# Keys and values of a head pair as seven block products in a gated cross-attention kernel, with the projections placed by due dates

## The chip, the cores and the metric

The kernel runs on one core of a Trainium2 chip. The time is the device time of one execution in microseconds. A run of several executions gives a median. One further execution was taken with the hardware profiler: the page and the trace are of that execution. TensorE does the matmuls, VectorE and ScalarE the elementwise work, POOL is GpSimd, and SP issues most of the DMAs.

## The reference, cut to what matters

```python
# x (4, 256, 512), ctx (4, 1601, 512); 32 query heads, 8 key/value heads, head size 128; all fp32
xn = layernorm(x)
q = (xn @ Wq + bq)                        # 4 query heads to one key/value head
k, v = split(ctx @ Wkv + bkv)             # 8 heads of 128 each
attn = softmax(q k^T / sqrt(128))
x = x + tanh(g_xattn) * (attn v @ Wo + bo)
x = x + tanh(g_ffn) * ffn(layernorm(x))   # base product, router over 8 experts, two rank-16 experts a token
```

## The kernel before

The work is a list of 4 x 8 key/value heads, `heads`. A head has two *groups*, `(b, h, l)`: group l holds 128 of the 256 tokens for the head's four query heads, 512 columns in all. The 1601 context tokens are 13 row tiles: twelve of 128 and one of 65. They are handled as seven "pairs", the short tile first.

**A group.** `run_group(cur, prev)` scores the current group and weights the values of the previous one, in turn. `score_unit` (L442) multiplies `kT` with `qT` into a score bank `sc`, and ScalarE copies it to a tile `p` (L449); `fold` keeps a running maximum on VectorE (L389 to L394). `av_unit` (L492) multiplies the exponentials of the previous group with `v` into the one bank `av`; at its end VectorE and ScalarE write `oT` (L502, L503). `AHEAD` says how many units the scores lead the values. After the group `softmax` spreads the maximum over the partitions (`spread`, L396 to L415), subtracts it on VectorE in seven instructions (L464) and takes the exponential on ScalarE (L465). The sums of the exponentials (`sum_unit`, again `fold` and `spread`) belong to the next call of `run_group`.

**Between two groups** comes what this document calls a *window*: the work that is not attention proper. Keys of a head come in four chunks of 400 or 401 tokens, four contraction blocks of 128 each (`pk`, L311), evacuated by ScalarE with the bias (L318). Queries come in four items (`pq`, L330, L337). Values of a head pair are made tile by tile, 256 columns for the two heads (`pv`, L363, L370). The output projection `po` (L515) follows its group and is added to `xa` by VectorE (L522). At the change of a batch the context is loaded and transposed into `ctxT` (L145, L146), and the feed-forward steps run.

**The order.** TensorE's order is the program's order (`manual_schedule`); other engines are ordered by a scheduler that looks at which instruction is ready and, among those, at which comes first in the program. A small planner writes TensorE's order. Work is cut into steps with a cost in ns and a lag before they may run (`LAG_O`, 6 us, between a group and its `po`). A `Task` is a list of such steps. `run_group` slips in steps of at most 432 ns (transposes) between units; `fill(share)` runs steps in list order until a share of all open cost is used up, 1/2 after the first group of a head and all after the second; `flush` then finishes what the next head needs.

**Memory.** PSUM has three score banks (`ps_sc`), one for `av` and four for all else (`ps`, `bank()`). `p` has `NPAIR + AHEAD + 1` = 10 buffers. `wk` is loaded twice ahead, `wv`, `wq` and `wo` once; loads wait on the SP queue for their buffer.

Of the kernel before, what the change touches and what calls it, by code (L numbers as in the profile page):

```python
# [27 lines left out]
def flamingo_kernel(  # L28
# [35 lines left out]


    nc = tc.nc
    B, L, D = x.shape
# [15 lines left out]
    NPAIR = len(pairs)  # L83
    AHEAD = 2
    n_chunks = -(-LK // 512)
    base, extra = divmod(LK, n_chunks)
    chunks, s = [], 0
    for i in range(n_chunks):
# [6 lines left out]
    small = ctx.enter_context(tc.tile_pool(name="small", bufs=4))  # L95
    ps_sc = ctx.enter_context(tc.tile_pool(name="ps_sc", bufs=3, space=bass.MemoryType.PSUM))
    ps_av = ctx.enter_context(tc.tile_pool(name="ps_av", bufs=1, space=bass.MemoryType.PSUM))
    ps = ctx.enter_context(tc.tile_pool(name="ps", bufs=4, space=bass.MemoryType.PSUM))

# [70 lines left out]

    def load_wk(b, h, eng=nc.sync):
        k = pool.tile([P, NC, HDIM], F32, tag="wk", name=f"wk_{b}_{h}")
        eng.dma_start(
            k, wkv[:, h * HDIM : (h + 1) * HDIM].rearrange("(c p) f -> p c f", p=P)
        )
        w_t["k", b, h] = k

    def load_wv(b, hp, eng=nc.sync):
        v = pool.tile([P, NC, 2 * HDIM], F32, tag="wv", name=f"wv_{b}_{hp}", bufs=1)
        lo = KVD + hp * 2 * HDIM  # L180
        eng.dma_start(v, wkv[:, lo : lo + 2 * HDIM].rearrange("(c p) f -> p c f", p=P))
        w_t["v", b, hp] = v

# [48 lines left out]

    xa_t, xnT_t, ctxT_t = {}, {}, {}
    STAGE = 3

# [31 lines left out]
    def ctx_steps(b):  # L267

        staged = {}

        def load(i):
            s = pool.tile([P, D], F32, tag="stage", name=f"ctx_{b}_{i}", bufs=STAGE)
            nc.sync.dma_start(s[: rows[i]], ctx_kv[b, i * P : i * P + rows[i], :])
            staged[i] = s

        def begin():
            ctxT_t[b] = pool.tile([P, NC, LK], F32, tag="ctxT", name=f"ctxT_{b}", bufs=1)
            for i in range(STAGE - 1):
                load(i)

        def step(i):
            def run():
                if i + STAGE - 1 < KT:
                    load(i + STAGE - 1)
                turn_ctx(b, i, staged.pop(i))
            return NC * TR_COST, LAG_CTX, run

        return [(0, 0, begin)] + [step(i) for i in range(KT)]

# [11 lines left out]

    def qk_steps(b, h):
        def begin():
            qT_t[b, h] = pool.tile([P, G, L], F32, tag="qT", name=f"qT_{b}_{h}")
            kT_t[b, h] = pool.tile([P, LK], F32, tag="kT", name=f"kT_{b}_{h}")

        def k_item(s, n):
            def run():
                pk = bank(f"pk_{b}_{h}_{s}")
                for c in range(NC):  # L310
                    nc.tensor.matmul(  # L311
                        pk[:, :n],
                        w_t["k", b, h][:, c, :],
                        ctxT_t[b][:, c, s : s + n],
                        start=(c == 0),
                        stop=(c == NC - 1),
                    )
                nc.scalar.activation(  # L318
                    kT_t[b, h][:, s : s + n],
                    pk[:, :n],  # L320
                    AF.Identity,
                    bias=bias_of("k", h),
                )
            return NC * mm_cost(n), 0, run

        def q_item(g):
            def run():
                pq = bank(f"pq_{b}_{h}_{g}")
                for c in range(NC):
# [7 lines left out]
                nc.scalar.activation(  # L337
                    qT_t[b, h][:, g, :],
                    pq[:, :L],
                    AF.Identity,  # L340
                    bias=bias_of("q", h * G + g),
                )
            return NC * mm_cost(L), 0, run

        return [(0, 0, begin)] + [k_item(s, n) for s, n in chunks], [q_item(g) for g in range(G)]

    def v_steps(b, hp):

        WV = 2 * HDIM

        def v_begin():
            v_t[b, hp] = pool.tile([P, KT, 2, HDIM], F32, tag="v", name=f"v_{b}_{hp}")

        def v_item(i):
            n = 2 if i + 1 < KT and rows[i + 1] == P else 1
            r = rows[i]

            def run():
                pv = bank(f"pv_{b}_{hp}_{i}")
                for j in range(n):  # L360
                    s = (i + j) * P
                    for c in range(NC):
                        nc.tensor.matmul(  # L363
                            pv[:r, j * WV : (j + 1) * WV],
                            ctxT_t[b][:, c, s : s + r],
                            w_t["v", b, hp][:, c, :],
                            start=(c == 0),
                            stop=(c == NC - 1),
                        )
                nc.scalar.copy(  # L370
                    v_t[b, hp][:r, i : i + n].rearrange("p j t f -> p (j t f)"), pv[:r, : n * WV]
                )
            return n * NC * mm_cost(WV), 0, run

        starts, i = [], 0
        while i < KT:
            starts.append(i)
            i += 2 if i + 1 < KT and rows[i + 1] == P else 1
        return [(0, 0, v_begin)] + [v_item(i) for i in starts]


# [150 lines left out]
    def ffn_steps(b, l):  # L532
# [17 lines left out]
        def pick(p, tag):  # L550
# [6 lines left out]
            return v, oh  # L557

        def route_item():
            pm = bank(f"pm_{nm}")  # L560
            WR = E * R + E
            for c in range(NC):
                nc.tensor.matmul(
                    pm[:, :WR], box["xT"][:, c, :], ra[:, c, :], start=(c == 0), stop=(c == NC - 1)
                )
            py = bank(f"py_{nm}")
            for c in range(NC):
                nc.tensor.matmul(py, box["xT"][:, c, :], base_t[:, c, :], start=(c == 0), stop=False)  # L568
            box["py"] = py
            lm = pool.tile([P, WR], F32, tag="lm", name=f"lm_{nm}")  # L570
# [34 lines left out]

        def final_item():
            py = box["py"]
            nc.tensor.matmul(py, box["midT"], lb, start=False, stop=True)
# [6 lines left out]
            (NC * TR_COST, LAG_NORM, turn_item),  # L615
            (NC * (mm_cost(E * R + E) + mm_cost(D)), LAG_COPY, route_item),
            (TR_COST, LAG_ROUTE, mid_item),
            (mm_cost(D), LAG_COPY, final_item),
        ]

# [6 lines left out]
    class Task:  # L627


        def __init__(self, steps, head=None):  # L630
            self.steps = deque(steps)
            self.head = head
            self.ready = clock["now"] + self.steps[0][1]
# [49 lines left out]

    def fill(share):

        credit = share * sum(t.cost() for t in tasks)
        while tasks and credit > 0:
# [7 lines left out]
            else:  # L695
                break

    ctx.enter_context(tc.manual_schedule(engines={mybir.EngineType.PE}))
# [11 lines left out]
    load_first(0)  # L710
    load_wk(*heads[0], nc.scalar)
    load_first(1)
    load_small()
    load_first(2)
    load_first(3)
    load_wv(0, 0)
    xs = x_steps(0, 0)
# [4 lines left out]
    ctxT_t[0] = pool.tile([P, NC, LK], F32, tag="ctxT", name="ctxT_0", bufs=1)  # L722
    ks, qs = qk_steps(*heads[0])
    ks.pop(0)[2]()
    vs = v_steps(0, 0)
    vs.pop(0)[2]()
    ends = [s + n for s, n in chunks]
# [15 lines left out]
    for f in xs + vs + qs:  # L743
        f[2]()
    load_wk(*heads[1])
    load_wq(*heads[1])
    load_wo(*heads[0])
    tasks.append(Task(ffn_weight_steps()))

    prev = None  # L750
    for hi, (b, h) in enumerate(heads):
        if hi + 2 < len(heads):
            load_wk(*heads[hi + 2])
        nxt = heads[hi + 1] if hi + 1 < len(heads) else None
        if h % 2 == 0:
            if h + 2 < NKV:
                load_wv(b, h // 2 + 1)
            elif b + 1 < B:
                load_wv(b + 1, 0)
            halves = v_steps(b, h // 2 + 1) if h + 2 < NKV else []  # L760
        if nxt is not None:
            ks, qs = qk_steps(*nxt)
            if nxt[1] == 0:
                tasks.append(Task(x_steps(nxt[0], LAG_NORM), nxt))
                tasks.append(Task(ctx_steps(nxt[0]) + ks + qs + v_steps(nxt[0], 0), nxt))
            else:
                tasks.append(Task(ks + qs, nxt))
        if halves:
            n = len(halves) // 2 if h % 2 == 0 else len(halves)
            tasks.append(Task(halves[:n], nxt))  # L770
            halves = halves[n:]
        for l in range(NL):
            cur = (b, h, l)
            if cur == last:
                break
            fill(0)
            run_group(cur, prev)
            if prev is not None:
                tasks.insert(0, Task(out_steps(prev)))
            prev = cur  # L780
            if nxt is not None:
                fill(1.0 / (NL - l))
        flush(lambda t: t.head == nxt and nxt is not None)
        if hi + 2 < len(heads):
            load_wq(*heads[hi + 2])

# [56 lines left out]
```

## Time and profile before

| | |
|---|---|
| median of 3 runs | 2713.86 us (2712.91 to 2722.68) |
| the profiled execution | 2717.0 us, span 2715.2 us |
| clock granted to TensorE | 0.994 |
| scores L442, values' weighting L492 | 1664 passes each, mean 594 and 592 ns |
| keys L311, values L363, queries L330 | 1024, 1664 and 1024 passes |
| HBM | 104.52 MB moved, 38 GB/s |

A group's line in the profile gives line, engine, operation, output and inputs with shapes, count, then busy time and mean duration, then the engine's idle time just before these instructions and what ended it. A matmul's duration holds a drain that overlaps the next matmul, so durations of TensorE don't add up; starts do. Each fp32 matmul of the code appears as two passes in the trace, each with a weight load (PEld).

### The profile page before, as it was taken

The numbers are of one execution on the slowest core, as the hardware profiler recorded it, in microseconds if no ns is written. First come the engines' busy times: TensorE is split into PE (matmuls) and PEld (weight loads), VectorE is DVE, ScalarE is ACT, GpSimd is POOL, SyncE is SP. The second block draws the span as 40 slices with busy tenths as digits, with TensorE's granted clock in tenths as the row PEclk, the third lists the DMA queues.
The fourth block names the chain that finished last, engine by engine and source line by source line (L and its number), as shares of the span: only waits on it lengthen the run. The fifth ranks groups of instructions, "written<-read, shape, count | busy, mean of one in ns | idle before, by whom it ended". The sixth has DMA issues, their size and how long they took to land.

```text
span 2715.2 us, 22496 instructions
## 1 busy us (share of the span) xinstructions
PE 2672.2 (98%) x7997; PEld 1478.2 (54%) x7997; DVE 2006.6 (74%) x3093; ACT 1178.8 (43%) x1821; POOL 6.2 (0%) x21
## 2 busy tenths in 40 slices
PE   8999999999999999999999999999999999999998
PEld 6555555555655555555555555555555555555543
DVE  1977777786768777778676787787866768777787
ACT  2543443454444434435443444444544444434442
POOL 0000000000000000000000000000000000000000
PEclk9999999999999999999999999999999999999999
DMA  4110110112001101011200110110210011100000
GB/s 156 41 35 28 35 31 28 43 43 76 25 23 54 35 20 43 16 43 58 61 28 20 55 35 22 40 35 24 72 35 28 20 47 35 35 27 32 19 13 24
DMA packets 69800, 104.52 MB, mean 38 GB/s; under 512 B 3068, under 2 KB 27692, under 8 KB 69688
## 3 DMA queue, kind: packets, MB, share of 16 engines
q1 hardware_dynamic: 68808, 102.27, 11.7%
q8 instruction: 63, 1.03, 0.2%
q0 software_dynamic: 272, 0.53, 0.1%
q14 instruction: 49, 0.40, 0.1%
q10 hardware_dynamic: 608, 0.29, 0.0%
HBM read 100.98 MB, written 2.10 MB: 38 GB/s over the span
## 4 chain that ended last, share of the span: by engine, by line
PE 94%; DVE 4%; ACT 1%; DMA 1%; issue 0%; SPq 0%; DVEq 0%; ACTq 0%
PE sc L442 26%; PE av L492 24%; PE pv L363 13%; PE pk L311 12%; PE po L515 8%; PE pq L330 8%; DVE p L464 1%; ACT p L465 1%; PE py L568 1%; PE pt_ctx L145 0%; DVE mx L394 0%; DMA ctx<-in_ctx_dram 0%; DVE p_last L464 0%; DVE mx L399 0%; DVE res_mx L413 0%
## 5 line engine op out<-in xcount | busy, mean ns | idle before, releaser
L442 PE MATMUL sc<-qT,kT 128*128 128x512 f32 (+1 forms) x1664 | 769.9, 594 | 6.2 <-ACT p_last L449 3.4
L492 PE MATMUL av<-p,v 65*128 65x512 f32 x1640 | 755.7, 592 | 0.0
L449 ACT COPY p<-sc 65x512 f32<-65x512 f32 x820 | 478.9, 585 | 598.5 <-PE sc L442 598.1
L394 DVE TENSOR_TENSOR mx<-mx,p 128x1024 f32<-128x1024 f32 x252 | 308.3, 1223 | 406.3 <-ACT p L449 405.8
L492 PEld LDWEIGHTS av<-p,v 65*128 65x128 f32 x1640 | 310.0, 190 | 382.3 <-issue 377.5
L442 PEld LDWEIGHTS sc<-qT,kT 128*128 128x128 f32 (+1 forms) x1664 | 307.4, 186 | 381.8 <-issue 359.3
L464 DVE TENSOR_TENSOR p<-p,res_mx 65x512 f32<-65x512 f32 x442 | 472.2, 1135 | 0.1
L465 ACT ACTIVATE p<-p 65x512 f32<-65x512 f32 x442 | 420.0, 989 | 34.0 <-DVE p L464 28.5
L311 PE MATMUL pk<-ctxT,wk 128*128 128x400 f32 (+1 forms) x1024 | 361.8, 506 | 8.5 <-ACT ctxT L146 7.1
L363 PE MATMUL pv<-wv,ctxT 128*128 128x256 f32 (+1 forms) x1664 | 369.1, 379 | 0.0
L363 PEld LDWEIGHTS pv<-wv,ctxT 128*128 128x128 f32 (+1 forms) x1664 | 308.9, 186 | 60.0 <-issue 13.1
L394 DVE TENSOR_TENSOR sm<-sm,p 128x1024 f32<-128x1024 f32 x252 | 307.9, 1222 | 17.0
L311 PEld LDWEIGHTS pk<-ctxT,wk 128*128 128x128 f32 x1024 | 195.5, 192 | 171.1 <-issue 28.6
L515 PE MATMUL po<-wo,oT 128*128 128x512 f32 x512 | 238.3, 609 | 15.2 <-ACT p L465 7.2
L330 PE MATMUL pq<-xnT,wq 128*128 128x256 f32 x1024 | 231.3, 379 | 0.0
L330 PEld LDWEIGHTS pq<-xnT,wq 128*128 128x128 f32 x1024 | 194.6, 190 | 47.8 <-issue 15.4
L503 ACT ACTIVATE oT<-oT,biasT 128x512 f32<-128x512 f32 x64 | 46.2, 722 | 363.8 <-DVE oT L502 363.8
L389 DVE TENSOR_TENSOR mx<-p,p 128x1024 f32<-128x1024 f32 x63 | 76.1, 1208 | 157.0 <-ACT p L449 157.0
L370 ACT COPY v<-pv 128x512 f32<-128x512 f32 (+1 forms) x112 | 61.6, 550 | 253.1 <-PE pv L363 253.1
L515 PEld LDWEIGHTS po<-wo,oT 128*128 128x128 f32 x512 | 99.2, 195 | 125.8 <-issue 96.5
L318 ACT ACTIVATE kT<-pk,biasT 128x400 f32<-128x400 f32 (+1 forms) x128 | 75.2, 587 | 133.2 <-PE pk L311 133.2
L337 ACT ACTIVATE qT<-pq,biasT 128x256 f32<-128x256 f32 x128 | 59.2, 463 | 73.9 <-PE pq L330 73.9
(108 smaller groups left out, 1145.2 us busy)
## 6 DMA issues: line engine op xcount, KB each, us to landing
wq<-in_L_xattn_Wq_dram SPq DMA_DIRECT2D x32, 1024.0 KB, 5.2
wo<-in_L_xattn_Wo_dram SPq DMA_DIRECT2D x32, 1024.0 KB, 5.1
ctx<-in_ctx_dram SPq DMA_DIRECT2D x48, 256.0 KB, 2.7
wv<-in_L_xattn_Wkv_dram SPq DMA_DIRECT2D x16, 512.0 KB, 3.3
wk<-in_L_xattn_Wkv_dram SPq DMA_DIRECT2D x31, 256.0 KB, 3.1
xa<-in_x_dram SPq DMA_DIRECT2D x4, 512.0 KB, 4.1
out_dram<-y SPq DMA_DIRECT2D x8, 256.0 KB, 2.0
base<-in_L_ffn_base_W_dram SPq DMA_DIRECT2D x4, 256.0 KB, 8.3
```

The lines of the kernel that those rows point to most:

```text
L311: nc.tensor.matmul(pk[:, :n], w_t["k", b, h][:, c, :], ctxT_t[b][:, c, s : s + n], start=(c == 0), stop=(c == NC - 1),)
L318: nc.scalar.activation(kT_t[b, h][:, s : s + n], pk[:, :n], AF.Identity, bias=bias_of("k", h),)
L330: nc.tensor.matmul(pq[:, :L], w_t["q", b, h][:, c, g * HDIM : (g + 1) * HDIM], xnT_t[b][:, c, :], start=(c == 0), stop=(c == NC - 1),)
L363: nc.tensor.matmul(pv[:r, j * WV : (j + 1) * WV], ctxT_t[b][:, c, s : s + r], w_t["v", b, hp][:, c, :], start=(c == 0), stop=(c == NC - 1),)
L389: nc.vector.tensor_tensor(acc, p[first], p[first + 1], op)
L394: nc.vector.tensor_tensor(acc, acc, p[j], op)
L442: nc.tensor.matmul(sc[:r, :], kT_t[b, h][:, i * P : i * P + r], qT_t[b, h][:, :, l * P : (l + 1) * P], start=True, stop=True,)
L449: nc.scalar.copy(p[:r, k, :], sc[:r, :])
L464: nc.vector.tensor_tensor(p, p, mb[:r].unsqueeze(1).to_broadcast([r, n, W]), ALU.subtract)
L465: nc.scalar.activation(p, p, AF.Exp, scale=scale)
L492: nc.tensor.matmul(av, v_t[b, h // 2][:r, i, h % 2, :], p_t[key][j][:r, k, :], start=(j == 0 and k == 0), stop=(j == NPAIR - 1 and k == le ...
L515: nc.tensor.matmul(po, oT_t[key][:, g, :], w_t["o", b, h][:, g, :], start=(g == 0), stop=(g == G - 1),)
```

## The change

For the pairs of heads of keys and of values, the two contraction halves (256 of 512), two heads and two halves of the first 1536 tokens (768 each) form a 2 x 2 block product. It is computed in Winograd's form of Strassen's algorithm with seven block products. The sums of weight blocks are made on GpSimd (`weight_sums`), the sums of context blocks on VectorE once a batch (`ctx_sums`, partly in place in `ctxT`). Each product runs on two pieces of 384 tokens, 28 matmuls of 384 columns for keys, 84 matmuls of 128 columns for values. A piece has three PSUM banks: x collects products 1, 6, 5, 3 one after the other and is copied out by ScalarE after each; z holds product 2, y products 7 and 4, and VectorE adds them to what was copied. The last 65 tokens are done plainly in `tail`. Head 0, head 1 and the first pair of values keep the plain form.

The planner's tasks get a due group in place of a head: values of a pair in the window after its own first group, queries mostly in the last window before their head, keys of the next pair spread over three windows (two where a batch begins). `window(now)` gives each task its cost divided by the windows left. Weights of a pair share one buffer `wkv`, loaded by four DMAs. `AHEAD` goes from 2 to 1, the score banks from 3 to 2, `ps` from 4 banks to 5, the staging buffers from 3 to 2. The base product of the feed-forward moves from `route_item` to `final_item` except in the last batch.

```diff
-    AHEAD = 2
+    AHEAD = 1
+    HK = FULL // 2 * P
+    NSUB = -(-HK // 512)
+    SUB = HK // NSUB
+    TAIL = 2 * HK
...
-    ps_sc = ctx.enter_context(tc.tile_pool(name="ps_sc", bufs=3, space=bass.MemoryType.PSUM))
+    ps_sc = ctx.enter_context(tc.tile_pool(name="ps_sc", bufs=2, space=bass.MemoryType.PSUM))
...
-    ps = ctx.enter_context(tc.tile_pool(name="ps", bufs=4, space=bass.MemoryType.PSUM))
+    ps = ctx.enter_context(tc.tile_pool(name="ps", bufs=5, space=bass.MemoryType.PSUM))
...
+    def load_pair(kind, b, hp, tile_=None, eng=nc.sync):
...
+            w = pool.tile([P, 7, 2, HDIM], F32, tag="wkv", name=f"w{kind}_{b}_{hp}", bufs=1)
+        lo = (KVD if kind == "v" else 0) + hp * 2 * HDIM
+        for slot, half, f in ((A11, 0, 0), (A12, 1, 0), (A21, 0, 1), (A22, 1, 1)):
+            eng.dma_start(
...
+    def weight_sums(kind, b, hp):
+        w = w_t[kind, b, hp]
+        for out_, x_, y_, op in (
+            (S1, A21, A22, ALU.add),
+            (S2, S1, A11, ALU.subtract),
+            (S4, A12, S2, ALU.subtract),
+            (S3, A11, A21, ALU.subtract),
+        ):
+            nc.gpsimd.tensor_tensor(w[:, out_], w[:, x_], w[:, y_], op)
...
-    STAGE = 3
+    STAGE = 2
...
+    def ctx_sums(b):
...
+        for s0 in range(0, HK, SUB):
...
+            nc.vector.tensor_tensor(t1, b12, b11, ALU.subtract)
+            nc.vector.tensor_tensor(t2, b22, t1, ALU.subtract)
+            nc.vector.tensor_tensor(t4, b21, t2, ALU.subtract)
+            nc.vector.tensor_tensor(b12, b22, b12, ALU.subtract)
+        nc.vector.tensor_tensor(tt, ct[:, 2:4, TAIL:], ct[:, 0:2, TAIL:], ALU.subtract)
...
+        kT_t[b, h] = pool.tile([P, LK], F32, tag="kT", name=f"kT_{b}_{h}", bufs=3)
...
+        v_t[b, hp] = pool.tile([P, KT, 2, HDIM], F32, tag="v", name=f"v_{b}_{hp}", bufs=1)
...
+        def product(i, s, bk, first):
+            if is_k:
+                for c in range(2):
+                    nc.tensor.matmul(
+                        bk[:, :SUB],
+                        a(SLOT[i], c),
+                        operand(i, c, s, SUB),
...
+            for t in range(SUB // P):
+                for c in range(2):
+                    nc.tensor.matmul(
+                        bk[:, t * HDIM : (t + 1) * HDIM],
+                        operand(i, c, s + t * P, P),
+                        a(SLOT[i], c),
...
+        def add_to(f, half, s, bk):
+            o = place(f, half, s)
+            nc.vector.tensor_tensor(o, seen(bk), o, ALU.add)
...
+                product(i, s, bk, i in (1, 2, 7))
+                if i == 1:
+                    copy_to(0, 0, s, bk)
+                elif i == 2:
+                    add_to(0, 0, s, bk)
+                elif i == 6:
+                    copy_to(1, 0, s, bk)
+                elif i == 5:
+                    copy_to(1, 1, s, bk)
+                    add_to(1, 1, s, banks["y", s])
+                elif i == 3:
+                    copy_to(0, 1, s, bk)
+                elif i == 4:
+                    add_to(1, 0, s, bk)
...
+        for i in (1, 2, 6, 7, 5):
+            steps += [step(i, s) for s in subs]
+        if n:
+            steps.append((2 * NC * mm_cost(P), 0, tail))
+        for i in (3, 4):
+            steps += [step(i, s) for s in subs]
...
-    def fill(share):
+    def window(now):
...
+        credit = sum(t.cost() / (t.due - now + 1 if t.due is not None else 1) for t in tasks)
...
+        flush(lambda t: t.due is not None and t.due <= now)
...
+            if h == NKV - 2 and l == 1 and b + 1 < B:
+                tasks.append(Task(x_steps(b + 1, LAG_NORM), now + 1))
+                tasks.append(Task(ctx_steps(b + 1), now))
             run_group(cur, prev)
             if prev is not None:
                 tasks.insert(0, Task(out_steps(prev)))
             prev = cur
+            if h % 2 == 0 and l == 0 and hi > 0:
+                tasks.append(Task(pair_steps("v", *pair), now))
+            if nxt is not None and l == (0 if h % 2 == 1 and nxt[1] > 0 else NL - 1):
+                tasks.append(Task(q_steps(*nxt), hi * NL + NL - 1))
+            if coming is not None and h % 2 + l == 1 and (l == 1) == (h < NKV - 2):
+
+                tasks.append(Task(pair_steps("k", *coming), (hi | 1) * NL + NL - 1))
             if nxt is not None:
-                fill(1.0 / (NL - l))
+                window(now)
+            if h % 2 == 0 and l == 0 and coming is not None:
+                load_pair("k", *coming)
+                weight_sums("k", *coming)
+            if h % 2 == 1 and l == NL - 1 and coming is not None:
+                load_pair("v", *coming)
+                weight_sums("v", *coming)
```

## The prediction

> **What bounds the kernel now.** I read the page's busy shares first, then the chain that ended last, then the groups by shape, then one undisturbed stretch of the timeline.
>
> ```profile
> span 2715.2 us, 22496 instructions
> PE 2672.2 (98%) x7997; PEld 1478.2 (54%) x7997; DVE 2006.6 (74%) x3093; ACT 1178.8 (43%) x1821; POOL 6.2 (0%) x21
> PE 94%; DVE 4%; ACT 1%; DMA 1%; issue 0%; SPq 0%; DVEq 0%; ACTq 0%
> ```
>
> TensorE is busy 98% of the span and is 94% of the chain. A gain can come only from fewer TensorE passes; a loss from TensorE being made to wait. Price of a pass: durations of matmuls contain a drain that overlaps the next one, so I take runs of equal instructions from the chain in order of time (start, length, what), and the groups for shapes.
>
> ```profile
> 53.59 6.92 PE pq L330 x32
> 201.13 8.63 PE pv L363 x40
> 232.09 8.07 PE pk L311 x24
> L311 PE MATMUL pk<-ctxT,wk 128*128 128x400 f32 x768 | 268.0, 499 | 1.7 <-DVE ctxT L146 1.4 <-ACT ctxT L146 0.3
> L363 PE MATMUL pv<-wv,ctxT 128*128 128x256 f32 x1536 | 340.8, 379 | 0.0
> L563 PE MATMUL pm<-ra,fT 128*128 128x136 f32 x64 | 8.9, 282 | 1.8 <-DVE fT L146 1.8
> L502 DVE TENSOR_TENSOR oT<-av,res_sm 128x512 f32<-128x512 f32 x64 | 41.9, 654 | 0.0
> ```
>
> A pass of 256 columns takes 8.63/40 = 215.8 ns, one of 400 takes 8.07/24 = 336.2: about 0.834 ns a column and 2.2 ns. Counts show two passes for each fp32 matmul of the code (1024 pk = 32 heads x 4 chunks x 4 blocks x 2).
>
> Next, a stretch between two groups, on TensorE and VectorE:
>
> ```profile
> 1013.59 5.31 PE L492 MATMUL av<-p,v 128*128 128x512 f32 x12
> 1018.74 5.34 PE L330 MATMUL pq<-xnT,wq 128*128 128x256 f32 x24
> ...
> 1027.37 3.60 PE L515 MATMUL po<-wo,oT 128*128 128x512 f32 x8
> ...
> 1020.46 7.48 DVE L464 TENSOR_TENSOR p<-p,res_mx 65x512 f32<-65x512 f32 x7
> 1027.86 1.21 DVE L389 TENSOR_TENSOR sm<-p,p 128x1024 f32<-128x1024 f32 x1
> ...
> 1032.38 0.74 DVE L522 SCALAR_TENSOR_TENSOR xa<-po,gates,xa 128x512 f32<-128x512 f32 x1
> 1039.40:1061.80 22.40, 22.40 (x54) 9.86 (x53) 10.49 (x16) 7.97 (x14) 0.00 (x0) 1.00 0.07 24
> ```
>
> When the last av pass of a group has been issued (1018.7), VectorE is occupied with the softmax until 1027.9, 9.1 us into the window; then come the sums. The xa addition, for a po that ended at 1030.8, is put between two sums: work of the window goes behind the subtractions but ahead of the sums. The last line is the following group (busy PE, PEld, DVE, ACT, POOL): VectorE is idle for 12 of its 22.4 us.
>
> Last, what a window costs when PSUM banks run out:
>
> ```profile
> 776.53 1.89 PE L330 MATMUL pq<-xnT,wq 128*128 128x256 f32 x8
> 780.83 3.67 PE L515 MATMUL po<-wo,oT 128*128 128x512 f32 x8 [2.41 <-ACT p L465]
> 773.04 7.48 DVE L464 TENSOR_TENSOR p<-p,res_mx 65x512 f32<-65x512 f32 x7
> 780.44 0.29 DVE L571 COPY lm<-pm 128x136 f32<-128x136 f32 x1
> ```
>
> pm, py, another py and pq held the four banks; their readers stood behind the seven subtractions and the exponentials, and TensorE stood for 2.41 us.
>
> **Passes saved.** Call the four windows of a head pair A, B (even head, l = 0, 1), C, D (odd head). Fifteen of sixteen pairs change, for keys and for values (head 0, head 1 and the first values stay plain).
>
> Keys, a pair: now 64 x 336.2 ns = 21.52 us. After: 7 products x 2 pieces x 2 blocks x 2 passes = 56 of 384 columns, 322.6 ns each by the line above, 18.07; the tail of 65 tokens is 8 matmuls, 16 passes, each bound by its 128-column weight load, which I put at 109: 1.74. Saved: 1.71.
>
> Values, a pair: now 104 x 215.8 = 22.44. After: 7 x 6 x 2 x 2 = 168 passes of only 128 columns, and 16 in the tail, each with a weight load of its own. By the line a pass is 109 ns: 20.06. Saved: 2.38.
>
> Together 4.09 us a pair, 61 us in 15 pairs.
>
> **A rule against it.** The short pass is the risk, because one weight load of 128 columns must hide behind 128 columns of matmul. The nearest row is pm, 136 columns with a load each: its eight passes begin at 726.44 and the next matmul at 727.36, 115 ns a pass, just what the line gives for 136. [...] At 115 the gain falls by 200 x 6 ns x 15 = 18 us, to 43. Nothing excludes a floor between.
>
> **What is added beside TensorE.** VectorE: six additions from PSUM a pair and kind, 128x384. From oT (654 ns at 512) and the folds (1214 at 1024), 1.09 ns a column: 514 ns each, 6.2 us a pair; ctx_sums 8 x 934 ns, 7.7 us a batch. In all 93 + 31 us: VectorE goes from 74% to about 79%. In the windows they delay the sums, which have the group's 12 idle us to end in. ScalarE: eight evacuations of 384 columns in place of eight of 400 or six of 512, and the tails: +1.5 us a pair at 43% load. POOL: four 128x256 operations a load, 30 loads; no row is near. [...]
>
> **Where stalls come.** The pool `ps` has five banks after the change, but a pair (products in the order 1, 2, 6, 7, 5, tail, 3, 4, each on two pieces) holds two x banks from product 1 to 3, two y banks from 7 to 4, and two z banks (product 2) until VectorE adds them. Times below count from the last av pass of the group before.
> - A, the values: products 1, 1, 2, 2, 6 fill 6.5 us, then comes po (its lag is 6 us), then the second 6; at 11.3 us product 7 wants a bank. The z additions can run from 9.1, the first is done by 9.7. No stall, 1.5 us of margin.
> - B: queries first (6.9), po, then five key steps (credit 6.6 us, 1.29 each). No stall.
> - C: key steps 6, 7, 7, 5, 5 (6.45 us), then po takes the fifth bank until 9.9; the tail wants one at once. VectorE leaves the subtractions at 9.1, adds both y (10.2), then xa (10.95): 1.1 us of stall. In 12 pairs: 13 us (the three keys loaded across a batch start in C instead).
> - D: the rest of the keys, then queries, which now come last before a group: L442 shows 0.56 us for a group that begins right behind qT (five times now). 15 x 0.56, less what is there: 7 us.
> - Batch change, three times: TensorE no longer waits for ctxT (2.05 + 0.28, L311 and L515 at 632 and 637): -7. ctx_sums stand before the sums, so the third score tile of group (7,0) waits for its p buffer (AHEAD 1, one buffer fewer): about 2 each, +6. The routing bank plus x and z banks in window A: 3.2 in place of 2.4, +2. Loads of ctx one ahead: 2.7 us to land against 3.9 between steps, hidden.
> - Score tiles in two banks: copy done 1.64 us after a score began, third one due at 1.72. 64 x 0.05 = 3.
> - Start and end: four issues in place of one on two queues, and p_last behind two banks: +2.
>
> Sum +26 us; 61 - 26 = 35. The profiled execution took 2717.0 us for its span of 2715.2, so it would take 2682. The median of the runs is 2713.86, 3.1 below it: 2679.
>
> **Rivals.**
> 1. All of the gain: the waits in C and D fall in other slots, and nothing new stalls: 61 us, 2653. For: the page shows TensorE without a gap in windows as short as 11.5 us. Against: the 2.41 us line.
> 2. Slower, by held banks. If the additions from PSUM are served behind the sums, not ahead of them, z and y stay held until some 21.5 us into A and C instead of 9.7: product 7 in A would stand 10 us, the tail in C 11. From 4.1 us a pair the gain is gone; with 8 us (served halfway) it is +59, 2773. For: readers stood 8 us behind the subtractions (lm). Against: xa at 1032.38 went ahead of the sums.
> 3. Little left: a pass costs 115 ns (a gain of 43) and the stalls are those above: -17, 2697; with 1 us in each of 60 windows in their place, +17, 2731. For: VectorE works through the whole of a window already (1014.4 to 1040.2), and gets more to do there. Against: the group after it gives it time.
> 4. The change does nothing: excluded, the passes are counted in the code.
>
> **How the numbers follow.** Forecast 0.50 (2664 to 2695), rival 1 0.20, rival 3 0.16 (0.08 of it at its good end, 0.06 within the bound, 0.02 slower), rival 2 0.14, a serial weight load being in it. A measurement of this kernel tells some 0.5%, 13.6 us, from no change. Faster 0.50 + 0.20 + 0.08 = 0.78, same 0.06, slower 0.14 + 0.02 = 0.16. The range runs from rival 1 with 5 us of today's stalls gone too, 2648, past the good end of rival 3 to 2708; rival 2 and the rest of 3, together 0.2, stay outside.
>
> **What would show it.** Right: 840 passes of 384 columns for keys and 2520 of 128 for values, runs of the latter at 109 ns; PE busy down by about 55; VectorE near 79%; idle time before the key tail of about 1 us, released by VectorE, and 0.56 before sc. Wrong: pv runs at 115 or more; idle before products 7 of the values; idle before L442 from ScalarE copies of several us a group.

## The result, and the profile after

The changed kernel takes 2752.86 us (median of 4 runs, 2752.24 to 2755.68). Beside it the kernel before took 2713.39 (2711.16 to 2722.68). The ratio is 1.0141, with an interval of 1.0116 to 1.0165: 1.4% slower, where 1.3% faster was forecast. First the page of the changed kernel: span, busy shares, and the chain that ended last by engine.

```profile
span 2750.8 us, 25888 instructions
...
PE 2653.8 (96%) x9317; PEld 1502.2 (55%) x9317; DVE 2149.1 (78%) x3309; ACT 1201.4 (44%) x1881; POOL 166.4 (6%) x141
...
PE 81%; DVE 15%; ACT 2%; issue 1%; DMA 0%; ACTq 0%; DVEq 0%
```

TensorE's share fell from 98% to 96%, and VectorE's part of the chain went from 4% to 15%. So TensorE now stands, and for VectorE. The waits of TensorE (who waits for whom; us in all, times, longest) say where:

```profile
PE ptk L550 <- DVE xa L721: 32.0, 12, 2.7
PE sc L641 <- ACT qT L361: 19.5, 19, 3.5
PE sc L641 <- ACT p L648: 8.0, 5, 3.3
...
PE ptk L550 <- ACT kT L552: 6.1, 15, 0.4
```

The first line, and 15 of the 19 waits of the second, are those that the prediction placed in windows C and D. The timeline of one window C, first TensorE, then VectorE (start, length, what, count, idle time before and who ended it):

```profile
481.57 3.60 PE L691 MATMUL av<-p,v 128*128 128x512 f32 x8
485.01 1.45 PE L455 MATMUL pxk<-T,wk 128*128 128x384 f32 x4
...
491.46 3.60 PE L714 MATMUL po<-wo,oT 128*128 128x512 f32 x8
497.73 1.10 PE L550 MATMUL ptk<-ctxT,wk 128*128 128x65 f32 x8 [2.67 <-DVE xa L721]
499.24 0.66 PE L550 MATMUL ptk<-ctxT,wk 128*128 128x65 f32 x4 [0.41 <-ACT kT L552]
499.73 0.71 PE L550 MATMUL ptk<-T,wk 128*128 128x65 f32 x4
500.24 2.87 PE L455 MATMUL pxk<-ctxT,wk 128*128 128x384 f32 x4
...
488.58 7.50 DVE L663 TENSOR_TENSOR p<-p,res_mx 65x512 f32<-65x512 f32 x7
496.00 1.01 DVE L498 TENSOR_TENSOR kT<-pyk,kT 128x384 f32<-128x384 f32 x2
496.93 0.74 DVE L721 SCALAR_TENSOR_TENSOR xa<-po,gates,xa 128x512 f32<-128x512 f32 x1
```

Read it from the last av pass, issued at 485.0. VectorE leaves the subtractions 11 us later, adds the two y banks, then reads `po` for `xa`; only then is there a bank for the tail. The order is the one forecast, and the wait is 2.67 us where 1.1 was forecast. Now compare the two groups of four `pxk` passes: 1.45 us at 485.01, 2.87 at 500.24. The second group ran at half the clock. The stretches around it (length, then busy PE, PEld, DVE, ACT, POOL with counts, the clock granted to TensorE, DMA share, GB/s):

```profile
493.30:496.70 3.40, 1.75 (x5) 0.45 (x3) 3.40 (x5) 3.40 (x5) 0.00 (x0) 1.00 0.22 17
496.70:500.10 3.40, 1.97 (x16) 1.83 (x16) 3.33 (x5) 0.84 (x2) 0.00 (x0) 1.00 0.78 293
500.10:503.50 3.40, 3.40 (x8) 1.73 (x7) 3.14 (x3) 0.67 (x2) 0.00 (x0) 0.50 0.00 0
503.50:506.90 3.40, 3.40 (x9) 1.42 (x8) 3.25 (x4) 1.98 (x4) 0.00 (x0) 1.00 0.00 0
```

One stretch of 3.41 us after the wait has a granted clock of 0.50. In the whole trace 12 of the 19 stretches at half clock stand just so behind the 12 waits of window C.

**Where the time went.** I priced every pass at 0.834 ns a column and 2.2 ns, and a pass of fewer than 128 columns as one of 128 (109 ns), as the prediction did, and summed what the distance from each start to the next holds beyond that. Passes: 2647.4 us before, 2586.0 after, 61.4 less. Excess, by the group and the window behind it (us in all):

| where | before | after | e1 | e5 | e9 | e4 |
|---|---|---|---|---|---|---|
| up to group 1 | 10.7 | 14.1 | 13.1 | 13.8 | 13.7 | 10.7 |
| A, 15 of them | -0.1 | 11.9 | 12.5 | 12.6 | 12.0 | 1.0 |
| B, 16 | 14.1 | 23.4 | 22.4 | 22.7 | 12.2 | 4.6 |
| C, 12 inside a batch | -0.1 | 58.6 | 0.8 | 0.8 | 2.0 | 0.8 |
| C, 3 at a batch's end | 15.0 | 6.7 | 5.1 | 6.4 | 5.8 | 0.1 |
| D, 15 | -0.1 | 19.4 | 28.2 | 19.0 | 10.2 | 1.0 |
| last two groups and the end | 19.1 | 20.8 | 20.7 | 21.5 | 19.0 | 20.8 |

The columns e1 to e9 are the experiments below. From before to after, the 61 us saved are met by some 97 us of new excess, 59 of them in the twelve windows C. (The last 0.3 us or so of what the halved clock costs there falls into row D: the next group's first score starts at 502.9 us, and the stretch ends at 503.5.)

### The profile page after: what moved, and what is told of

It is laid out like the page before. It is cut to its first block, busy times and chain, and to the rows that moved or that the text cites. A ratio compares the mean times of both kernels' runs of the same rounds, so it can differ in the third digit from the quotient of the medians.

```text
span 2750.8 us, 25888 instructions
## 1 busy us (share of the span) xinstructions
PE 2653.8 (96%) x9317; PEld 1502.2 (55%) x9317; DVE 2149.1 (78%) x3309; ACT 1201.4 (44%) x1881; POOL 166.4 (6%) x141
## 4 chain that ended last, share of the span: by engine, by line
PE 81%; DVE 15%; ACT 2%; issue 1%; DMA 0%; ACTq 0%; DVEq 0%
PE sc L641 26%; PE av L691 22%; PE pq L354 7%; DVE p L663 5%; PE po L714 5%; PE pxv L466 5%; PE pxk L455 4%; PE pyv L466 2%; PE pyk L455 2%; DVE mx L593 1%; PE ptk L550 1%; PE pzv L466 1%; PE pzk L455 1%; PE py L761 1%; ACT p L664 1%
## 5 line engine op out<-in xcount | busy, mean ns | idle before, releaser
L641 PE MATMUL sc<-qT,kT 128*128 128x512 f32 (+1 forms) x1664 | 796.6, 604 | 32.1 <-ACT qT L361 19.5
L691 PE MATMUL av<-p,v 65*128 65x512 f32 x1640 | 766.6, 593 | 1.6 <-ACT p L664 1.6
L663 DVE TENSOR_TENSOR p<-p,res_mx 65x512 f32<-65x512 f32 x442 | 473.2, 1138 | 2.0
L593 DVE TENSOR_TENSOR sm<-sm,p 128x1024 f32<-128x1024 f32 x252 | 314.9, 1250 | 18.4
L209 POOL TENSOR_TENSOR wv<-wv 128x256 f32<-128x256 f32 x60 | 103.4, 1744 | 1612.0 <-DMA wv<-in_L_xattn_Wkv_dram 1610.8
L209 POOL TENSOR_TENSOR wk<-wk 128x256 f32<-128x256 f32 x60 | 56.8, 967 | 789.0 <-DMA wk<-in_L_xattn_Wkv_dram 687.2
L490 ACT ACTIVATE kT<-pxk,biasT 128x384 f32<-128x384 f32 x120 | 68.4, 570 | 76.1 <-PE pxk L455 76.1
L455 PE MATMUL pxk<-ctxT,wk 128*128 128x384 f32 x240 | 100.0, 558 | 0.0
L494 ACT COPY v<-pxv 128x384 f32<-128x384 f32 x120 | 56.0, 472 | 85.6 <-PE pxv L466 85.3
L466 PEld LDWEIGHTS pxv<-wv,T 128*128 128x128 f32 x720 | 84.9, 192 | 7.2 <-issue 7.2
L466 PE MATMUL pxv<-wv,T 128*128 128x128 f32 x720 | 87.2, 275 | 0.0
```

Of the source, the lines that this page charges most:

```text
L209: nc.gpsimd.tensor_tensor(w[:, out_], w[:, x_], w[:, y_], op)
L455: nc.tensor.matmul(bk[:, :SUB], a(SLOT[i], c), operand(i, c, s, SUB), start=first and c == 0, stop=c == 1, skip_group_check=True,)
L466: nc.tensor.matmul(bk[:, t * HDIM : (t + 1) * HDIM], operand(i, c, s + t * P, P), a(SLOT[i], c), start=first and t == 0 and c == 0, stop=c ...
L593: nc.vector.tensor_tensor(acc, acc, p[j], op)
L641: nc.tensor.matmul(sc[:r, :], kT_t[b, h][:, i * P : i * P + r], qT_t[b, h][:, :, l * P : (l + 1) * P], start=True, stop=True,)
L663: nc.vector.tensor_tensor(p, p, mb[:r].unsqueeze(1).to_broadcast([r, n, W]), ALU.subtract)
```

## Experiments

**e1: the tail behind products 3 and 4.** It asks whether window C is the loss.

```diff
-        for i in (1, 2, 6, 7, 5):
+        for i in (1, 2, 6, 7, 5, 3, 4):
             steps += [step(i, s) for s in subs]
         if n:
             steps.append((2 * NC * mm_cost(P), 0, tail))
-        for i in (3, 4):
-            steps += [step(i, s) for s in subs]
```

> Theory (fifth bank, then the clock): in twelve C windows the key tail waits 2.67 us for the bank that po holds, and the granted clock is halved for 3.41 us after it, which costs 1.7 us more. With the tail behind products 3 and 4, x banks are free when it comes: both go, 12 x 4.4 = 52 us, so about 2700 us, below the kernel before; the clock's dips at those places vanish. Rival (VectorE, 78% busy, is the bound inside windows): the wait only moves to product 4 or to the next score, and the time stays within 10 us of 2753.

Measured: 2701.29 us (2700.57 to 2705.73), 0.9963 of before (0.9949 to 0.9977), 51.6 below the changed kernel. The wait on `xa` and all twelve stretches at half clock are gone. What is left:

```profile
PE sc L639 <- ACT qT L361: 19.5, 19, 3.5
PE sc L639 <- ACT p L646: 7.2, 5, 3.3
PE ptk L550 <- ACT kT L552: 6.1, 15, 0.4
PE pyk L455 <- DVE kT L498: 5.8, 6, 1.6
```

A pair of heads took 163.81 us and takes 159.18: 4.63 us for a wait that the list of waits shows with 2.67. Most of the rest is the halved stretch, since 3.41 us at half clock cost 1.71. So one placement made the change slower, and without it the kernel is some 0.4% faster than before. That gain is clear of these runs' noise (the interval ends at 0.9977), but smaller than the 0.5% that the prediction took as the least that can be told from no change.

**e2: the output product behind the tail instead of ahead of it.** The same bank is freed by holding `po` back in window C.

```diff
-        return [(G * mm_cost(D), LAG_O, project)] + ...
+        lag = 9000 if h % 2 == 0 and l == 1 else LAG_O
+        return [(G * mm_cost(D), lag, project)] + ...
```

> Same wait taken away from the other side: in C the lag of po is 9 us in place of 6, so po comes behind the tail and one piece of product 3. Theory: the tail finds its bank, po finds one freed by the tail; about 2700 to 2710 us (up to 0.5 us of wait may stay at po). Rival (the order of products, not the bank, matters): no change, 2753.

Measured: 2791.45 us (2790.39 to 2794.32), ratio 1.0291 (1.0276 to 1.0306): a miss by over 80 us, and 39 worse than the changed kernel. The first line of its waits, then lines of the timeline of one window C:

```profile
PE ptk L550 <- ACT kT L552: 61.5, 15, 5.0
```

```profile
499.01 2.95 ACT L664 ACTIVATE p<-p 128x1024 f32<-128x1024 f32 x3
...
501.87 0.30 ACT L552 ACTIVATE kT<-ptk,biasT 128x65 f32<-128x65 f32 x1
...
502.21 1.12 PE L550 MATMUL ptk<-ctxT,wk 128*128 128x65 f32 x4 [5.02 <-ACT kT L552]
```

The two halves of the tail share a bank, and ScalarE's copy of the first half stands ahead of the second. With the tail placed early that copy falls behind the exponentials: 5.02 us in place of 0.41, and then 6.8 us at half clock. The small line `ptk <- ACT kT` of the changed kernel had been short only because the large wait came first.

**e3: two units ahead again.** `AHEAD` decides how many av passes follow a group's last score, so when the softmax starts in the window.

```diff
-    AHEAD = 1
+    AHEAD = 2
```

> AHEAD 2 in place of 1 alone, with 10 p buffers. Six av products in place of four follow the last score, so VectorE's softmax starts 1.72 us earlier against the window. Theory: the wait before the key tail falls from 2.67 to about 1 us, short enough that the clock is not halved in those places; 12 x (1.7 + 1.7) = 41 us and a few at the batch changes: about 2710 us. Rival (the wait comes from the place of the sums): the wait stays at 2.67 and the time at 2753.

Measured: 2777.61 us (2776.25 to 2780.93), ratio 1.0240 (1.0225 to 1.0255). VectorE in window C, then the waits:

```profile
482.61 7.47 DVE L663 TENSOR_TENSOR p<-p,res_mx 65x512 f32<-65x512 f32 x7
490.01 0.55 DVE L498 TENSOR_TENSOR kT<-pyk,kT 128x384 f32<-128x384 f32 x1
490.48 1.21 DVE L588 TENSOR_TENSOR sm<-p,p 128x1024 f32<-128x1024 f32 x1
491.61 0.55 DVE L498 TENSOR_TENSOR kT<-pyk,kT 128x384 f32<-128x384 f32 x1
492.08 0.74 DVE L721 SCALAR_TENSOR_TENSOR xa<-po,gates,xa 128x512 f32<-128x512 f32 x1
```

```profile
PE ptk L550 <- DVE xa L721: 23.1, 12, 1.9
PE po L714 <- ACT qT L361: 18.3, 3, 6.1
PE ptk L550 <- ACT kT L552: 15.7, 15, 3.6
...
PE po L714 <- DVE lm L775: 9.3, 3, 3.1
```

The last av pass is issued at 480.9 here, so the subtractions end 9.1 us into the window, just the figure of the prediction, which took it from a trace with `AHEAD` at 2. In the changed kernel it is 11.0. But the wait is still 1.93, not 1.1, because a sum (1.21 us) slips in between the two y additions: with the softmax done earlier, the sum is ready before the second addition, for which ScalarE has still to copy the second piece of product 5 (from 490.10 us on, for 0.57). The batch changes get worse (the lines with 6.1 and 3.1 us), and the whole is 25 us above the changed kernel where 43 below was expected.

This run also separates the halved clock from the wait. Of its twelve waits of 1.93 us in C, eight are followed by a halved stretch and four are not. Two of them, one of each kind, each with the stretch in which the wait ends and the next:

```profile
328.10:331.50 3.40, 1.47 (x5) 0.40 (x3) 3.40 (x6) 2.09 (x3) 0.00 (x0) 1.00 0.17 30
331.50:334.90 3.40, 2.99 (x19) 2.48 (x20) 3.30 (x4) 0.63 (x2) 0.00 (x0) 1.00 0.73 279
...
491.80:495.20 3.40, 1.93 (x15) 1.79 (x16) 3.33 (x5) 0.32 (x1) 0.00 (x0) 1.00 0.88 269
495.20:498.60 3.40, 3.40 (x8) 1.76 (x8) 3.23 (x4) 0.63 (x2) 0.00 (x0) 0.51 0.10 39
```

From the tail of a window with a halved stretch to the next tail is 163.12 us, from one without 161.43. The halved stretch alone costs 1.69 us. It follows the stretch that has fewer idle microseconds (1.47, against 1.93) but holds the tail's narrow passes as well; the last section comes back to this.

**e4: the banks and `AHEAD` alone, in the kernel before.** The buffers of PSUM and the lead of the scores, without the seven products; the staging buffers stay at 3.

```diff
-    AHEAD = 2
+    AHEAD = 1
...
-    ps_sc = ctx.enter_context(tc.tile_pool(name="ps_sc", bufs=3, space=bass.MemoryType.PSUM))
+    ps_sc = ctx.enter_context(tc.tile_pool(name="ps_sc", bufs=2, space=bass.MemoryType.PSUM))
...
-    ps = ctx.enter_context(tc.tile_pool(name="ps", bufs=4, space=bass.MemoryType.PSUM))
+    ps = ctx.enter_context(tc.tile_pool(name="ps", bufs=5, space=bass.MemoryType.PSUM))
```

> The kernel before with the change's buffers alone: AHEAD 1, two score banks, five other banks. Theory: the buffers cost little where nothing holds banks through a window: 2713 within 8 us (the 2.41 us wait for a bank at three places goes, or grows with the later softmax). Rival (two score banks and the shorter lead make the loss by themselves): 20 us or more above, 2735 or more.

Measured: 2698.44 us (2697.74 to 2700.04), ratio 0.9947 (0.9933 to 0.9962). A gain of about 15 us, more than either theory had. Its page, and the first of its waits:

```profile
PE 2667.5 (99%) x7997; PEld 1469.6 (55%) x7997; DVE 2009.5 (75%) x3093; ACT 1192.1 (44%) x1821; POOL 6.2 (0%) x21
```

```profile
PE po L515 <- ACT oT L503: 5.7, 2, 4.9
```

The wait of 2.41 us that the prediction showed at a batch change (`po <- ACT p`) is gone: the longest wait left for `po` stands at the end of the program. The waits of `pk` for `ctxT` at the batch changes (2.05 us) are gone too, and with both went the five halved stretches that the trace of before had at 632, 1301, 1451, 1977 and 2124 us. Whether the banks or the lead did it was not tried apart. So e1, with the seven products, is no faster than the buffers by themselves (2701 and 2698): what is left of its waits eats the saved passes.

**e5: e1, and the tail's copies after both halves.**

```diff
-                if is_k:
-                    nc.scalar.activation(kT_t[b, h0 + f][:, TAIL:], ...)
-            if not is_k:
+            if is_k:
+                for f in range(2):
+                    nc.scalar.activation(kT_t[b, h0 + f][:, TAIL:], ...)
+            else:
```

> On e1: both evacuations of the key tail stand behind both of its halves, so the second half no longer waits for ScalarE to read the bank the two share. Theory: 15 waits of 0.41 us go, about 2695 us. Rival (such a short wait is made up elsewhere): 2701.

Measured: 2692.97 us (2691.20 to 2694.60), ratio 0.9920 (0.9905 to 0.9935), 8.3 below e1. The 15 waits of 0.41 are gone.

**e6: e1, with `ctx_sums` ten microseconds later.** It asks whether the context's sums cause the 3.5 us wait for `qT` before group (7,0).

```diff
-        return [(0, 0, begin)] + [step(i) for i in range(KT)] + [(0, 0, lambda: ctx_sums(b))]
+        return [(0, 0, begin)] + [step(i) for i in range(KT)]
...
+            if h == NKV - 1 and l == 0 and b + 1 < B:
+                tasks.append(Task([(0, 10000, lambda b=b: ctx_sums(b + 1))], now))
```

> On e1: ctx_sums of the next batch is emitted 10 us into group (7,0), where VectorE idles, in place of amid the softmax of group (6,1). Theory: at three batch changes qT waits 3.5 us behind exponentials that wait for a delayed softmax, and the clock is halved there; both fall to the usual 0.56: 3 x (2.9 + 1.7) = 14 us, about 2687. Rival (the short window before group (7,0) alone makes that wait): under 5 us.

Measured: 2703.83 us (2701.24 to 2706.40), ratio 0.9962 (0.9948 to 0.9976); the wait is unchanged. A miss; the rival, under which the short window makes the wait, holds. ScalarE in that window:

```profile
609.68 5.46 ACT L662 ACTIVATE p<-p 65x512 f32<-65x512 f32 x6
615.04 0.82 ACT L361 ACTIVATE qT<-pq,biasT 128x256 f32<-128x256 f32 x2
```

The last two items of the queries are copied behind six exponentials. The window is short, and the queries come last in it.

**e7: e1, with the output product last in every window D,** so that it covers the copies of `qT`.

```diff
+        lag = 8500 if h % 2 == 1 and l == 0 else LAG_O
```

> On e1: in window D po has a lag of 8.5 us, so that po and not the last query item stands ahead of the next group. Theory: 12 waits of 0.56 us for qT go: 7 us, about 2694. Rival: po last holds up its own addition and so nothing on TensorE, same gain; or a bank is missing for it: a loss.

Measured: 2714.20 us (2713.27 to 2715.96, 12 runs), ratio 0.9999 (0.9991 to 1.0008), 13 above e1. Twelve of the `qT` waits went, as expected. In the three windows D at a batch's end, where the next batch's first keys have only two windows, another took their place. Its waits, its timeline on TensorE, and the stretches (columns as above):

```profile
PE pyk L455 <- DVE kT L498: 16.1, 6, 5.0
```

```profile
1347.46 1.45 PE L455 MATMUL pyk<-T,wk 128*128 128x384 f32 x4
1353.94 2.93 PE L455 MATMUL pyk<-T,wk 128*128 128x384 f32 x4 [5.03 <-DVE kT L498]
```

```profile
1349.40:1352.80 3.40, 0.00 (x0) 0.00 (x0) 3.40 (x4) 3.32 (x4) 0.00 (x0) 1.00 0.00 0
1352.80:1363.10 10.30, 8.76 (x23) 6.01 (x24) 9.33 (x11) 2.32 (x4) 0.00 (x0) 0.50 0.09 24
```

Product 4 wants a y bank that VectorE adds only behind its subtractions; `po` had stood in between. Three waits of 5 us with up to 10 us of half clock each cost more than twelve of 0.56 without.

**e8: e5, e6 and e7 together, and the bias loaded ahead of the weights.**

> All of these together, and at the start the bias loads issued ahead of the four key-weight loads on ScalarE's queue (TensorE waits 3.7 us for the bias there). Theory: the waits are independent, 6 + 14 + 7 + 3 = 30 us below e1, about 2671 us, 1.6% below the kernel before. Rival (a wait removed comes back at the next scarce bank): no better than the best of the three, 2687.

Measured: 2702.89 us (2701.22 to 2704.18), ratio 0.9958 (0.9946 to 0.9971). A miss by 32 us, for the reasons of e6 and e7, whose waits both stand in its list (16.1 and 12.8 us). At the start the wait for the bias went (3.7 us in e1), but that for `ctx` was 8.4 us where e1 had 4.8: no gain.

**e9: e5, the output product last only where that covers something, and the queries of head 1 in the first window.**

```diff
+        late = l == 0 and (h == NKV - 2 if h % 2 == 0 else h < NKV - 1)
+        return [(G * mm_cost(D), 8500 if late else LAG_O, project)] + ...
...
-            if nxt is not None and l == (0 if h % 2 == 1 and nxt[1] > 0 else NL - 1):
+            if nxt is not None and l == (0 if hi == 0 or h % 2 == 1 and nxt[1] > 0 else NL - 1):
...
-                tasks.append(Task(q_steps(*nxt), hi * NL + NL - 1))
+                tasks.append(Task(q_steps(*nxt), now if hi == 0 else hi * NL + NL - 1))
```

> e1 with the evacuations after both halves, and two edits. First, the output product stands last in the D windows only where the next head is of the same batch, and in the C window at the batch change (head 6), where the queries of the next head waited 3.5 us. Second, the query product of head 1 is moved into window 0, where the scores waited 3.25 us for ScalarE. Theory (each wait that goes takes its own length and, if it is over some 2 us, the halved stretch of about 1.7 us with it): 2693 - 12 x 0.56 - 3 x (3.4 + 1.7) - 5 = about 2666, range 2655 to 2678, and the queries' wait on ScalarE (19.5 us in e1) falls under 5. Rival (the output product moved behind the last batch window's queries makes another product wait there, as it did in e7, where product 4 came to wait 5.0 us): 2690 to 2705 and a new wait of over 2 us, three times, in the chain.

(The text on record says "the C window at the batch change"; by the prediction's names it is the last pair's window B.) Measured: 2672.55 us (2672.20 to 2673.07), ratio 0.9852 (0.9837 to 0.9866): 41 us faster than before, 80 faster than the changed kernel, 26 faster than the buffers alone. Its page and its first waits:

```profile
PE 2621.4 (98%) x9317; PEld 1491.6 (56%) x9317; DVE 2145.1 (80%) x3309; ACT 1195.9 (45%) x1881; POOL 189.6 (7%) x141
```

```profile
PE sc L640 <- ACT qT L361: 8.9, 8, 2.2
PE pyk L455 <- DVE kT L498: 7.5, 6, 1.6
PE sc L640 <- ACT p L647: 5.7, 7, 1.2
```

The same 9317 passes as the changed kernel, with TensorE at 98%. Until the last 110 us of the span no stretch at half clock is left; the granted clock is 0.997, where the changed kernel had 0.988. The `qT` waits fell from 19.5 us to 8.9, not to under 5, so part of the gain expected there stayed out: 2673 and not 2666. The table places what e9 gains on e5: 10.5 us in the windows B, the three at a batch's end and the first of all, and 8.8 in the windows D.

**e10: e5 with plain keys,** to see what the keys' seven products are worth.

```diff
         steps = [(0, 0, begin)]
+        if is_k:
+            return steps + plain_k_steps(b, h0) + plain_k_steps(b, h0 + 1)
...
-                weight_sums("k", *coming)
+                pass
```

> e1 with the evacuations after both halves, and the keys of each batch taken plainly (eight block products instead of seven, no sums of weights for them); the values keep their seven products. It leaves out: the keys of tokens 768 to 1535 are formed from a block that the sums of the context have overwritten with a difference, so these keys are not the reference's. Theory (the seven products are worth their passes also for the keys once their waits are gone): 24 passes a pair of 384 columns and less are added, 25.7 us of passes in all, and the waits around products 4 and the output at the batch changes go (12 us with their halved stretches): about 2712, range 2703 to 2720. Rival (the values alone carry the gain, and the keys' seven products give back in waits what they save): 2693 or less.

Measured: 2710.06 us (2708.60 to 2712.63, 20 runs), ratio 0.9988 (0.9981 to 0.9995), 17.1 above e5. The passes add 25.7, and the waits that go with the keys' products give a third of it back. (The text on record counts 24 passes a pair more; they are 8 fewer, 9197 in all against 9317, but of 400 columns.) The theory is borne out; the rival (2693 or less) is not. The values' seven products were not tried by themselves.

## Why the prediction was wrong

- **Passes saved: right.** 61.4 us by the prediction's own prices, 61 forecast. A key product's pass costs 322.7 ns (322.6 forecast). A value product's is a little dearer:

```profile
413.63 2.84 PE L466 MATMUL pxv<-wv,T 128*128 128x128 f32 x24
416.31 1.47 PE L550 MATMUL ptv<-wv,ctxT 128*65 128x128 f32 x12
```

  24 passes in 2.68 us are 111.7 ns each, where the line gave 109 and rival 3 took 115: 2.7 ns on 2520 passes, 7 us. PE's busy time fell by 18 us, not 55, mostly since a halved stretch counts as busy (3.40 of 3.40 us in the one shown at 500.1); in e9 it fell by 51. The serial weight load, which rival 2's chance has in it, no run shows: the 24 loads of these passes span 2.76 us, although one alone has 192 ns in the trace (mean), and the passes follow each other every 111.7 ns. In which way the loads are hidden here, no run shows.
- **Work on other engines: right in kind.** VectorE is at 78% (79 forecast), additions take 541 to 546 ns (514 forecast). The trace of before had no row near GpSimd's operations; they take 967 ns for keys and 1744 for values, and no wait of TensorE is released by them. The groups by shape:

```profile
L209 POOL TENSOR_TENSOR wv<-wv 128x256 f32<-128x256 f32 x60 | 103.4, 1744 | 1612.0 <-DMA wv<-in_L_xattn_Wkv_dram 1610.8
...
L209 POOL TENSOR_TENSOR wk<-wk 128x256 f32<-128x256 f32 x60 | 56.8, 967 | 789.0 <-DMA wk<-in_L_xattn_Wkv_dram 687.2 <-PE av L691 100.5
...
L498 DVE TENSOR_TENSOR kT<-pyk,kT 128x384 f32<-128x384 f32 x60 | 30.8, 545 | 0.4
```

- **"C: ... 1.1 us of stall. In 12 pairs: 13 us": the step that failed.** Place, number and releaser were right; e1 shows the cost as 51.6 us. Of the 71 us by which the new excess passes the 26 forecast, 46 stand in the row of these twelve windows. Two terms were wrong, by 19 and by 20 us in twelve windows. The wait was 2.67 us: the window's clock ("VectorE leaves the subtractions at 9.1") was read from the trace of before, where two units of scores lead, and was not moved when the change set `AHEAD` to 1. With one unit fewer behind the last score, four av matmuls follow it, not six, and the softmax ends 1.9 us later in the window (e3 puts the 9.1 back). The other term was missing altogether: each of these waits is followed by 3.41 us at half clock, 1.7 us each. The trace of before had five such stretches, and the prediction priced none of them.
- **D: right in kind.** 0.56 us before the scores in each of these windows, as forecast (the list has 19 waits for `qT`; one is at the start, three are those of 3.5 us below). From start to start each costs 0.73 us (539.61 to 540.55, less the 0.22 of the pass itself), and with these, the tail's waits at a batch's end and the rest of the halved clock, row D holds 19 us, not 7. The tail's second half (0.41 us, 15 times, 12 of them in C) was not in the sum. A and B had no wait inside a batch, as forecast.
- **"Batch change": right in sign only for the credit.** The credit of 7 us left out the halved stretches behind these waits: in e4 row C at a batch's end falls by 14.9 us. In the changed kernel it falls by 8.3, as 6.7 us of other excess stands there. The wait for the routing bank, forecast to grow from 2.4 to 3.2 us, went; in its window the scores wait 1.4 us for ScalarE, three times. The feared wait of +6 at group (7,0) from `ctx_sums` did not come; a wait of 3.5 us for `qT`, three times, came in the same place, from ScalarE's order (e6).
- **Start: wrong.** +2 was given for start and end. The stretch up to group 1 took 3.4 us more. The window behind group 1, where the scores waited 3.25 us for ScalarE and 6.8 us then ran at half clock, has 6.9 us of excess, and had none before. e9 moved work there, and it is quiet.
- **The rivals.** Rival 1 (nothing new stalls) is out. Rival 3's pass of 115 ns is out at 111.7. Rival 2 (held banks) named the right resource and the right engine, but its condition was not met: the additions did go ahead of the sums. The loss came through the forecast's own mechanism at four times its price. In the last stages (e9) the kernel reaches 2673, near the forecast's 2679. That is in part luck: some 15 us of it came with the buffers (e4), where the forecast gave a credit of 7, and it describes these products with their waits removed, not the change as made.

## What to carry to other kernels

On a kernel that TensorE bounds, price a wait with what it does to the clock, and look what stands beside it: here each wait of 2.67 us, with narrow passes right behind it, cost 1.7 us more. When a change shifts how far one stage leads another, every time read "from the window's start" in the old trace must be moved with it. And try buffers and algorithm apart: the buffers alone were worth 15 us here, and one held bank hid what the algorithm saves. Before a product is moved to cover one wait, ask which wait it has been covering.

## What the runs showed of the hardware

- In the changed kernel's trace the clock stood at half in 19 stretches: 17 of 3.41 us, one of 6.83 at 93.9 us, and one of 3.30 that ends with the program. All 19 begin on one grid of 3.41 us pieces. The starts at 172.423, 336.262 and 500.103 us lie 48 pieces apart. That alone could be the program's own period, since a pair of heads takes 163.81 us, just 48 pieces, so that every window C met the grid in nearly the same place, which is luck. But the stretches behind other waits, at 1305.65 and 2705.11 us, lie on the same grid, 332 and 742 pieces after the first. In the trace of before the eight halved stretches begin on one such grid too (632.08 and 1301.09 us lie 196 pieces apart).
- Waits of 2.67 us were followed by a halved stretch every time (12 of 12 in the changed kernel), and waits of 1.93 us eight times of twelve in e3. Waits of 0.56 us brought none in the changed kernel, nor did those of 1.50 us at e9's batch changes.
- Idle time alone does not tell which. Of the changed kernel's stretches shown above, 493.30:496.70 has 1.65 us without a matmul and is followed by full clock; 496.70:500.10 has 1.43 and is followed by half. The second holds the tail's 16 passes of 65 columns, some 112 ns apart, of which the columns fill 54 ns (0.834 a column). So I counted, for every piece of these grids at full clock in the traces of the kernel before and of the changed kernel (without the first 20 and the last 100 us of each), the time that columns do not fill: 3.41 us less 0.834 ns for each column of its passes. Of 1480 pieces with under 2.05 us unfilled, none was followed by a halved one; of 18 with over 2.15, every one was; of the nine between, three. The two windows of e3 shown above agree: where the clock halved, the wait shares a piece with 15 of the tail's passes (491.80:495.20, some 2.6 us unfilled); where it did not, the wait and the tail fall into two pieces (some 2.1 and 1.6). This is read off the traces: no run varied the unfilled share by itself.
- GpSimd took 967 ns in one place and 1744 in another for the same 128x256 operation, and 2120 in e9 (means). In the changed kernel's trace, 17 of the 120 operations ran while VectorE did nothing and took 0.72 to 0.73 us; the eleven longest, 3.1 to 3.7 us, ran beside 2.7 to 3.2 us of VectorE's subtractions of the maximum (L663). No run took this neighbour away.
- Passes of 128 columns with a load of 128x128 weights each ran at 111.7 ns, one after the other (the 24 of the changed kernel from 413.63 us on).
